# A graph attention layer on one core: twenty places for the turns of the gathers, six of them behind VectorE and ScalarE

## The chip, the cores and the metric

The kernel runs on one core of a Trainium2 chip. A core has TensorE (PE, matrix products; PEld is its weight load), VectorE (DVE), ScalarE (ACT), GpSimd (POOL) and SyncE (SP), each with its own stream of instructions; they wait for each other on semaphores. Sixteen DMA engines move data between HBM and the core's memories, SBUF and PSUM. The metric is the device time of one launch in microseconds (us).

## What is computed

A graph of 12500 nodes with 256 features and 200000 edges, sorted by destination. The layer norm of each node, cut at zero, is `h`. Queries, keys and values with 8 heads are taken from `h`; each edge gets a logit per head, a softmax runs over the edges of a destination, and the weighted values are summed there. A skip product, a GELU, a second layer norm and two residual sums follow.

```python
h = jnp.maximum(_layernorm(x, axis=-1), 0.0)
q = (h @ Wq + bq).reshape(n, HEADS, D)          # k, v alike
logits = jnp.einsum('ehd,ehd->eh', q[dst], k[src]) / jnp.sqrt(jnp.float32(D))
seg_max = jax.ops.segment_max(logits, dst, num_segments=n)
expv = jnp.exp(logits - seg_max[dst])
attn = expv / jax.ops.segment_sum(expv, dst, num_segments=n)[dst]
agg = jax.ops.segment_sum(attn[:, :, None] * v[src], dst, num_segments=n)
out = agg.reshape(n, HID) + (h @ Wskip + bskip)
y = h + jax.nn.gelu(out, approximate=False)
return x + (y - mu) / jnp.sqrt(var + 1e-05) * gamma + beta
```

## The kernel before

A first phase makes `h` and a table `kv_tab` in HBM with a row of 512 numbers for each node, 256 of its key and 256 of its value, and the tables that describe the edges. Then comes the walk over the edges, which takes nearly all of the time. It has NST = 64 steps; a step `c` works on S = 8 streams of edges with K = 3 tiles of 128 edges each (the last step has one tile). The pipeline is written out by hand in one loop body: in the turn of the loop that belongs to step `c`, the last tile of step `c` and the first two of step `c + 1` get their logits, the softmax of step `c` is taken, its values are weighed and added up, and the queries of step `c + 2` are made.

The pieces that the prediction speaks of:

- `turn_windows` (L1493 on TensorE, L1497 on ScalarE) turns the windows of `h` that hold the destinations of a step, and copies them to `hwT`; `queries` (L1511, L1514) multiplies them by the query weights and copies the product to `qw`.
- `spread` (L1585) spreads queries over the edges of a tile, half of its streams at a time, into a PSUM tile with two buffers; `times` (L1596, VectorE) multiplies them with the gathered keys in place; `total` (L1603) sums over a head; `turn` (L1622) transposes the logits; `maxima` (L1634 to L1638) takes the running maxima of the segments and the exponentials.
- `weigh` (L1670, VectorE) multiplies the gathered values by the weights; `hot_n` (L1572, L1575) makes the matrix that sorts edges to nodes, `to_n`; `add_up` (L1693) multiplies the two into sums per node. ScalarE's `taken` (L1716, L1720) copies these out, one group of streams after another.
- `dense` handles one much used group of nodes beside the walk in steps 2 to 50 (L1865 to L1914; its `often` is L1898), and `Pair` finishes 256 nodes in a step, from step 15 on (L1224 to L1335; `shifted` is L1314 and L1317, `scale` is L1321 and L1323). SyncE issues the plain loads and stores.

On each engine the order of the program is kept by `keep`, which hangs every instruction on the one before it on its engine, kept in `latest`. The gathers of GpSimd are not kept so. A tile `(c, j)` of gathered keys and values needs eight of them, one a stream; each is an indirect DMA of 128 rows of `kv_tab`. `gather_next(c, j)` takes a buffer (there are six) for tile `(c + 2, j)` and puts its eight rows on a list, `waiting`. It is called at the start of the loop body for the last tile of the step before, and after `weigh(c, 0)` and `weigh(c, 1)`. A call of `turns` takes rows off the list, in order, and issues each with a semaphore wait on the instruction that it is given: the gather's turn. So a gather can't start before that instruction has ended, and GpSimd, which runs in order, holds all later gathers as well.

Before the change `turns` is called in the pieces themselves, always with TensorE's latest instruction, and the number of rows stands in small tables there: `(1, 2)[part]` in `turn_windows`, `(0, 1)[part]` in `queries`, `(1, 0, 0, 2)[i]` in `hot_e`, `(1, 0, 1)[j]` in `hot_n`, `((1, 1), (1, 2), (1, 1))[j][half]` in `spread`, `(2, 2, 1)[j]` in `turn` and one in each of the three finished groups of `add_up`. In the steady loop that makes turns for just the 24 rows of a step, and two rows of a step's second tile are left for the next step.

Of the kernel before, what the change touches and what calls it, by code (L numbers as in the profile page):

```python
# [37 lines left out]
ACT = mybir.EngineType.Activation  # L38
PE = mybir.EngineType.PE
# [1086 lines left out]
def walk_streams(tc, N, HID, NST, KL, many, ident, idx, d0_row, slot_row, less, near_n, e_tab, at_tab, pen_tab, h_tab,  # L1126
# [268 lines left out]
    with ExitStack() as es:  # L1395
# [90 lines left out]
        def turn_windows(c, part):  # L1486

            g = step[c]
            tiles = (range(1), range(1, 3))[part]
            ps = hot_ps.tile([P, 2, KC, P], F32, name="ps_hot")[:, :len(tiles)]  # L1490
            for r, i in enumerate(tiles):
                for k in range(KC):
                    keep(nc.tensor.transpose(ps[:, :, k, r::2] if part else ps[:, 0, k, :],  # L1493
                                             g["hw"][:, i, k * P:(k + 1) * P], ident))
            turns(latest[PE], (1, 2)[part])
            g["hwT"] = hold.tile([P, 2, KC, P], F32, name="hwT", bufs=1)[:, :len(tiles)]
            keep(nc.scalar.copy(g["hwT"], ps))  # L1497

        def queries(c, part):

            g = step[c]
            if part == 0:
                g["qw"] = hold.tile([P, 3, HID], F32, name="qw")
            tiles = (slice(0, 1), slice(1, 3))[part]
            n = tiles.stop - tiles.start
            ps = hot_ps.tile([P, 2, HID], F32, name="ps_hot")[:, :n]
            keep(nc.tensor.matmul(ps, one_row, twice(b_q3, n), start=True, stop=False,
                                  skip_group_check=True))
            for b in range(n):
                for k in range(KC):  # L1510
                    keep(nc.tensor.matmul(ps[:, b, :], g["hwT"][:, b, k, :], w_q[:, k, :],  # L1511
                                          start=False, stop=k == KC - 1, skip_group_check=True))
            turns(latest[PE], (0, 1)[part])
            keep(nc.scalar.copy(g["qw"][:, tiles, :], ps))  # L1514

        def gather(c, j, behind=None):
# [18 lines left out]
                mybir.DependencyClass.Sync, mybir.DependencyReason.DATA),  # L1535
                reason="turn of the gathers")

        def turns(behind, n=1):

            for _ in range(n):  # L1540
                if waiting:
                    gather_row(*waiting.pop(0), behind)

        def gather_next(c, j):

# [5 lines left out]
        def hot_e(c, i):  # L1551

            g = step[c]
            if i == 0:
                g["to_e"] = hot.tile([P, S // 2, CH], F32, name="to_e")
            turns(latest.get(PE), (1, 0, 0, 2)[i])
            if i % 2:
                t = g["to_e"][:, i - 1:i + 1, :]
                keep(nc.scalar.activation(t, t, AF.Relu, scale=-1.0, bias=ones))  # L1559
                return  # L1560
            for k, pairs in ((0, slice(0, 1)), (1, slice(1, 2))) if i == 0 else ((2, slice(2, 4)),):
                keep(nc.scalar.activation(g["to_e"][:, pairs, :], g["at"][:, pairs, :], AF.Square,  # L1562
                                          bias=less[:, k:k + 1]))

        def hot_n(c, j):

            n = near_n.shape[1]
            if j == 0:
                step[c]["to_n"] = (hot.tile([P, K, n], F32, name="to_n", bufs=1) if c < NST - 1
                                   else done[0].spare(n)[:, None, :])  # L1570
            ps = hot_ps.tile([P, S * WN], F32, name="ps_hot")[:, :n]
            keep(nc.tensor.matmul(ps, step[c]["et"][:, j * P:(j + 1) * P], near_n, start=True,  # L1572
                                  stop=True))
            turns(latest[PE], (1, 0, 1)[j])
            keep(nc.scalar.activation(step[c]["to_n"][:, j, :], ps, AF.Relu, scale=-1.0,  # L1575
                                      bias=ones))

        def spread(c, j, half):

            g = step[c]  # L1580
            ps = qe_ps.tile([P, 2, 2, HID], F32, name="ps_qe")
            for a in range(2):
                for b in range(2):
                    r = slice(b * WN, (b + 1) * WN)
                    keep(nc.tensor.matmul(ps[:, b, a, :],  # L1585
                                          g["to_e"][r, 2 * half + a, j * P:(j + 1) * P],
                                          g["qw"][r, (half + a) * half, :], start=True, stop=True))
            g["qe", half] = ps
            turns(latest[PE], ((1, 1), (1, 2), (1, 1))[j][half])

        def times(c, j, half):

# [22 lines left out]
        def turn(c, j):  # L1615

            g = step[c]
            if c == NST - 1:
                g["xt"] = ag_ps.tile([P, 2 * HID], F32, name="ps_a")
            else:  # L1620
                g["xt"] = logits
            keep(nc.tensor.transpose(g["xt"][:SH, j * P:(j + 1) * P], g["L"][:, j, :], ident))  # L1622
            turns(latest[PE], (2, 2, 1)[j])
            if j == 0:
                keep(nc.scalar.copy(g["xt"][:SH, 0:1],
                                    low0 if c == 0 else step[c - 1]["M"][:, CH - 1:]))
# [52 lines left out]
        def add_up(c, i, tiles=range(K), later=None):  # L1679

            g = step[c]
            streams = [s for s in range(S) if where(s)[0] == i]
            if tiles[0] == 0 and i == 0 and c > NST - 3:
                g["ps", i] = (bank(2)() if c == NST - 2 else logits)[:, :SUMS]
            elif tiles[0] == 0:
                g["ps", i] = (hot_ps.tile([P, 2 * HID], F32, name="ps_hot")
                              if i == 1 or i == 2 and c > NST - 3 else
                              ag_ps.tile([P, 2 * HID], F32, name="ps_a"))[:, :SUMS]
            ps = g["ps", i]
            for j in tiles:  # L1690
                for s in streams:
                    _, at, w = where(s)
                    keep(nc.tensor.matmul(ps[at:at + w, :],  # L1693
                                          g["to_n"][:, j, i * P + at:i * P + at + w],
                                          g["vw"][j][:, s, :], start=j == 0,
                                          stop=j == tiles_of(c) - 1, skip_group_check=True))
            if tiles[-1] < tiles_of(c) - 1:
                return
            turns(latest[PE])
            if later is not None:  # L1700
                later.append((c, i))
            else:
                taken(c, i)
# [343 lines left out]
        for c in range(NST - 1):  # L2047
# [75 lines left out]
                gather_next(c - 1, K - 1)  # L2123
            times(c, K - 1, 0)
            times(c, K - 1, 1)
            if a:
                a.turn()
            if before:
# [2 lines left out]
            if before:  # L2131
                before.shifted()
            total(c, K - 1)
            spread(c + 1, 0, 0)
            spread(c + 1, 0, 1)
            if c == ONCE[1]:
                ending = dense_rows(c)
                next(ending)
            turn_windows(c + 2, 0)
            next(ending, None)  # L2140
            if before:
                before.scale()
                before.store(0)
            turn(c, K - 1)
            if a:
                a.logits()
            behind_exp = []
            if c:
                add_up(c - 1, 0, range(K - 1, K), behind_exp)
            if c:  # L2150
                add_up(c - 1, 1, later=behind_exp)
            if pair:
                pair.turn(later=True)
            maxima(c)
# [4 lines left out]
            turn_back(c)  # L2159
            if c:  # L2160
                add_up(c - 1, 2)
            if a:
                a.top()
                a.exps()
# [3 lines left out]
            if pair:  # L2168
                pair.divisors()
            hot_n(c, 1)  # L2170
            times(c + 1, 0, 0)
            spread(c + 1, 1, 0)
            if a:
# [6 lines left out]
                pair.fetch_x()  # L2180
            times(c + 1, 0, 1)
            hot_n(c, 2)
            total(c + 1, 0)
            if a:
                a.often()
# [2 lines left out]
            if pair:  # L2188
                pair.divide()
            spread(c + 1, 1, 1)  # L2190
            next(ending, None)
            if a:
                a.sums()
# [6 lines left out]
            if pair:  # L2200
                pair.skip(1)
            times(c + 1, 1, 0)
            times(c + 1, 1, 1)
            turn(c + 1, 0)
            spread(c + 1, K - 1, 0)
            queries(c + 2, 0)
            total(c + 1, 1)
            weigh(c, 1)
            gather_next(c, 1)
# [5 lines left out]
            if ahead:  # L2215
                ahead.load()
            turn_windows(c + 2, 1)
            if c + 3 < NST:
                prefetch(c + 3)
            if pair:  # L2220
# [1 line left out]
                table_of(EXP)  # L2222
            next(ending, None)
            turn(c + 1, 1)
            if pair:
                pair.stats(pair.ps)
            weigh(c, K - 1)
            queries(c + 2, 1)
            hot_e(c + 2, 1)
            next(making, None)  # L2230
            spread(c + 1, K - 1, 1)
            hot_e(c + 2, 2)
            if pair:
                pair.root()
# [488 lines left out]
```

## Time and profile before

| | |
|---|---|
| runs | 2621.85, 2622.62, 2644.91 us; median 2622.62 |
| profiled execution | 2633.05 us, its span 2631.5 us |
| granted TensorE clock, mean | 0.853 |
| DMA queue of the gathers (q0): packets, MB, share of 16 engines | 125472, 410.09, 53.2% |
| DMA queue of SyncE (q1): packets, MB, share | 126736, 188.13, 22.8% |
| HBM | 228 GB/s over the span |

The profile is of one execution and somewhat above the median of the runs; sums are made against its own time. Its lines name the line of the kernel, the engine, the operation and the tiles, out<-in. An engine counts as busy while it runs an instruction, not while it waits or issues. Matmuls overlap each other, and their ends in the profile are modelled.

### The profile page before, as it was taken

What the parts mean: (1) busy time and instruction counts of PE and PEld (TensorE: products, weight loads), DVE (VectorE), ACT (ScalarE), POOL (GpSimd) and SP (SyncE); (2) the same over time, 40 slices, a digit from 0 to 9 for tenths busy, and PEclk for the clock granted to TensorE, in tenths of its full rate; (3) what the DMA queues carried; (4) which work ended last, traced back from release to release, by engine and by line L of the source; (5) the groups of instructions that cost most, each with busy time, mean ns of one, the idle gap of its engine ahead of it and who ended that gap; (6) DMA issues with size and microseconds to landing.
All of it is one profiled execution on the core that took longest, in us unless ns stands there. A gap on an engine that the chain in (4) does not pass through costs nothing. (4 is left out here: it accounts for less than half of the span.)

```text
span 2631.5 us, 37655 instructions
## 1 busy us (share of the span) xinstructions
PE 2026.1 (77%) x10723; PEld 1236.4 (47%) x10723; DVE 1905.2 (72%) x2326; ACT 1208.9 (46%) x2667; POOL 1569.9 (60%) x1732
## 2 busy tenths in 40 slices
PE   9994667777777877777787877777777777767776
PEld 4443444444444544554455544544454444444443
DVE  8885766666667777777777777777777776767675
ACT  5662234333333545454545454545454544444443
POOL 5435666666666656666666566565666565666664
PEclk9997787777787889888888888898899888878888
DMA  9786777777767877887787777887788787778773
GB/s 349 292 279 196 211 212 214 213 217 216 213 205 221 232 226 225 234 243 231 230 233 233 232 230 233 242 234 226 235 235 237 229 234 217 226 222 237 225 225 102
DMA packets 253648, 601.84 MB, mean 229 GB/s; under 512 B 53875, under 2 KB 101544, under 8 KB 250486
## 3 DMA queue, kind: packets, MB, share of 16 engines
q0 software_dynamic: 125472, 410.09, 53.2%
q1 hardware_dynamic: 126736, 188.13, 22.8%
q8 instruction: 88, 1.44, 0.2%
q10 hardware_dynamic: 1222, 1.11, 0.1%
q14 instruction: 130, 1.06, 0.1%
HBM read 517.70 MB, written 81.42 MB: 228 GB/s over the span
## 5 line engine op out<-in xcount | busy, mean ns | idle before, releaser
L1531 POOL DMA_INDIRECT kv<-kv_tab,idx x1472 | 1396.7, 949 | 886.5 <-issue 366.0
L1585 PE MATMUL ps_qe<-qw,to_e 64*128 64x256 f32 x3040 | 564.5, 477 | 123.3 <-issue 63.2
L1596 DVE TENSOR_TENSOR kv<-ps_qe,kv 128x1024 f32<-128x1024 f32 x380 | 451.3, 1217 | 171.7 <-remote 65.9
L1585 PEld LDWEIGHTS ps_qe<-qw,to_e 64*128 64x128 f32 x3040 | 359.2, 227 | 297.6 <-issue 196.4
L1670 DVE TENSOR_TENSOR vw<-ps_x,kv 128x2048 f32<-128x2048 f32 x188 | 427.0, 2271 | 56.3 <-ACT to_n L1575 16.6
L1603 DVE TENSOR_REDUCE L<-kv 128x64 f32<-128x2048 f32 x190 | 434.2, 2285 | 4.8
L1693 PE MATMUL ps_a<-vw,to_n 128*32 128x264 f32 (+1 forms) x2232 | 233.7, 434 | 82.9 <-issue 48.4
L1511 PE MATMUL ps_hot<-w_q,hwT 128*128 128x256 f32 x768 | 252.9, 477 | 24.3 <-ACT hwT L1497 11.0
L1514 ACT COPY qw<-ps_hot 128x256 f32<-128x256 f32 (+1 forms) x128 | 61.4, 480 | 433.9 <-issue 125.5
L1511 PEld LDWEIGHTS ps_hot<-w_q,hwT 128*128 128x128 f32 x768 | 165.6, 230 | 77.0 <-issue 22.3
L350 PE MATMUL ps_kv<-w_kv,hT 128*128 128x512 f32 x392 | 184.4, 594 | 0.7 <-ACT hT L264 0.7
L1693 PEld LDWEIGHTS ps_a<-vw,to_n 128*32 128x32 f32 (+1 forms) x2232 | 90.3, 126 | 179.1 <-issue 111.8
L1898 DVE TENSOR_TENSOR kv<-ps_hot,cnt 128x256 f32<-128x256 f32 x49 | 20.8, 425 | 201.7 <-PE ps_hot L1894 136.6
L1720 ACT COPY kv<-ps_a 1x264 f32<-1x264 f32 x372 | 137.3, 369 | 5.5
L1562 ACT ACTIVATE to_e<-at,less 128x384 f32<-128x384 uint8 (+1 forms) x192 | 130.8, 715 | 16.6 <-DMA et<-e_tab 16.6
L1622 PE MATMUL ps_x<-ident,L 128*64 128x128 f32 x189 | 59.6, 315 | 101.6 <-issue 81.4
L1572 PE MATMUL ps_hot<-near_n,et 48*128 48x384 bf16 x190 | 68.7, 386 | 83.9 <-remote 20.5
L1497 ACT COPY hwT<-ps_hot 128x256 f32<-128x256 f32 (+1 forms) x128 | 61.0, 477 | 142.4 <-PE ps_x L1622 59.7
L1435 ACT ACT_TABLE_LOAD x97 | 124.5, 1283 | 2.8 <-issue 1.1
L1575 ACT ACTIVATE to_n<-ps_hot,ones 128x384 f32<-128x384 f32 x189 | 108.2, 576 | 34.2 <-PE ps_hot L1572 24.4
L1693 PE MATMUL ps_hot<-vw,to_n 128*64 128x264 f32 x768 | 120.0, 456 | 3.3 <-issue 2.8
L1559 ACT ACTIVATE to_e<-to_e,ones 128x768 f32<-128x768 f32 x128 | 119.3, 932 | 0.7
(445 smaller groups left out, 2827.4 us busy)
## 6 DMA issues: line engine op xcount, KB each, us to landing
kv<-kv_tab,idx POOLq DMA_INDIRECT x1520
kv_tab<-kvo SPq DMA_DIRECT2D x23, 1024.0 KB
hw<-h_tab SPq DMA_DIRECT2D x256, 64.0 KB
table<-sums_w SPq DMA_DIRECT2D x252, 61.9 KB
group<-h_tab SPq DMA_DIRECT2D x49, 256.0 KB
sums<-table SPq DMA_DIRECT2D x94, 132.0 KB
at<-at_tab SPq DMA_DIRECT2D x64, 192.0 KB
h<-h_tab SPq DMA_DIRECT2D x94, 128.0 KB
```

The source lines that it names most:

```text
L350: nc.tensor.matmul(ps_kv, hT[:, c, :], w_kv[:, c, :], start=c == 0, stop=c == KC - 1)
L1435: keep(nc.scalar.preload_act_table_set(name))
L1511: keep(nc.tensor.matmul(ps[:, b, :], g["hwT"][:, b, k, :], w_q[:, k, :], start=False, stop=k == KC - 1, skip_group_check=True))
L1531: ins = nc.gpsimd.indirect_dma_start(out=t[:, s, :], out_offset=None, in_=kv_tab[:, :], in_offset=bass.IndirectOffsetOnAxis(ap=idx[:, s, j ...
L1559: keep(nc.scalar.activation(t, t, AF.Relu, scale=-1.0, bias=ones))
L1562: keep(nc.scalar.activation(g["to_e"][:, pairs, :], g["at"][:, pairs, :], AF.Square, bias=less[:, k:k + 1]))
L1585: keep(nc.tensor.matmul(ps[:, b, a, :], g["to_e"][r, 2 * half + a, j * P:(j + 1) * P], g["qw"][r, (half + a) * half, :], start=True, stop= ...
L1596: keep(nc.vector.tensor_tensor(k, g["qe", half].rearrange("p b a d -> p a b d"), k, op=OP.mult))
L1603: keep(nc.vector.tensor_reduce(g["L"][:, j, :].rearrange("p (s h) -> p s h", s=S), g["kv"][j][:, :, :HID].rearrange("p s (h d) -> p s h d" ...
L1670: keep(engine.tensor_tensor(t[:, :, HEADS:].rearrange("p s (h d) -> p s h d", h=HEADS), wj[:, :, :, None].to_broadcast([P, t.shape[1], HEA ...
L1693: keep(nc.tensor.matmul(ps[at:at + w, :], g["to_n"][:, j, i * P + at:i * P + at + w], g["vw"][j][:, s, :], start=j == 0, stop=j == tiles_o ...
L1720: keep(copy(step[c + 1]["kv"][0][0:1, s, HID - HEADS:], ps[at:at + 1, :]))
```

## The change

All calls of `turns` leave the pieces and stand in the body of the loop, in twenty places. `turns` now takes the engine and the number, and waits for the latest kept instruction of that engine.

```diff
@@ turn_windows, queries, hot_e, hot_n, spread, turn, add_up
-            turns(latest[PE], (1, 2)[part])
-            turns(latest[PE], (0, 1)[part])
-            turns(latest.get(PE), (1, 0, 0, 2)[i])
-            turns(latest[PE], (1, 0, 1)[j])
-            turns(latest[PE], ((1, 1), (1, 2), (1, 1))[j][half])
-            turns(latest[PE], (2, 2, 1)[j])
-            turns(latest[PE])
...
-        def turns(behind, n=1):
+        def turns(engine, n):
 
             for _ in range(n):
                 if waiting:
-                    gather_row(*waiting.pop(0), behind)
+                    gather_row(*waiting.pop(0), latest[engine])
@@ the loop
                 gather_next(c - 1, K - 1)
             times(c, K - 1, 0)
             times(c, K - 1, 1)
+            turns(DVE, 1)
...
             total(c, K - 1)
+            turns(DVE, 1)
             spread(c + 1, 0, 0)
             spread(c + 1, 0, 1)
...
             turn_windows(c + 2, 0)
+            turns(PE, 1)
+            turns(ACT, 1)
...
             turn(c, K - 1)
+            turns(PE, 1)
...
                 add_up(c - 1, 0, range(K - 1, K), behind_exp)
+                turns(PE, 2)
             if c:
                 add_up(c - 1, 1, later=behind_exp)
+                turns(PE, 1)
...
                 add_up(c - 1, 2)
+                turns(PE, 1)
...
             hot_n(c, 1)
+            turns(ACT, 1)
+            turns(PE, 1)
             times(c + 1, 0, 0)
             spread(c + 1, 1, 0)
...
             times(c + 1, 0, 1)
             hot_n(c, 2)
+            turns(PE, 1)
             total(c + 1, 0)
...
             gather_next(c, 0)
...
             spread(c + 1, 1, 1)
+            turns(PE, 2)
...
             times(c + 1, 1, 0)
+            turns(DVE, 1)
             times(c + 1, 1, 1)
             turn(c + 1, 0)
+            turns(PE, 1)
             spread(c + 1, K - 1, 0)
+            turns(PE, 1)
             queries(c + 2, 0)
+            turns(ACT, 1)
             total(c + 1, 1)
             weigh(c, 1)
             gather_next(c, 1)
...
             turn_windows(c + 2, 1)
+            turns(PE, 1)
...
             turn(c + 1, 1)
+            turns(PE, 2)
...
             queries(c + 2, 1)
+            turns(PE, 2)
...
             spread(c + 1, K - 1, 1)
+            turns(PE, 1)
```

They are numbered here in the order of the loop, 1 to 24, a call for two rows counting as two. Turns 1, 2 and 15 hang on VectorE, 4, 10 and 18 on ScalarE. In the steady loop turns 1 to 4 issue the last four rows of tile `(c + 1, 1)`, 5 to 12 those of `(c + 1, 2)`, 13 to 20 those of `(c + 2, 0)`, and 21 to 24 the first four of `(c + 2, 1)`; four rows are left for the next step instead of two.

## The prediction

> **What bounds the kernel now.** I read the page first, its totals and its groups by line. Columns of a group: busy us, mean ns of one, then the idle time of the engine just before it and what ended most of that.
>
> ```profile
> span 2631.5 us, 37655 instructions
> ...
> PE 2026.1 (77%) x10723; PEld 1236.4 (47%) x10723; DVE 1905.2 (72%) x2326; ACT 1208.9 (46%) x2667; POOL 1569.9 (60%) x1732
> ...
> L1531 POOL DMA_INDIRECT kv<-kv_tab,idx x1472 | 1396.7, 949 | 886.5 <-issue 366.0
> ...
> L1596 DVE TENSOR_TENSOR kv<-ps_qe,kv 128x1024 f32<-128x1024 f32 x380 | 451.3, 1217 | 171.7 <-remote 65.9
> ...
> L1898 DVE TENSOR_TENSOR kv<-ps_hot,cnt 128x256 f32<-128x256 f32 x49 | 20.8, 425 | 201.7 <-PE ps_hot L1894 136.6
> ```
>
> No engine is full. TensorE and VectorE are busy for three quarters and hand work to each other; VectorE's two largest waits are L1596 (171.7 us) and L1898 (201.7 us). GpSimd does nothing in the loop but gathers: 949 ns each, and it sat idle for 886.5 us before them. The question for this change is whether anything waits for a gather. The first reader of gathered data is `times`, L1596, so the second view is that line's own: what VectorE sat idle for before it (us, times).
>
> ```profile
>   remote: 65.9, 17
>   PE ps_qe L1585: 32.5, 10
>   PE ps_hot L1317: 26.7, 8
>   PE ps_hot L1865: 23.2, 9
>   PE ps_a L1693: 13.6, 8
>   issue: 9.3, 4
> ```
>
> These six make 171.2 of the 171.7 us. Four are TensorE, none is a gather or another DMA. "Remote" is a release by a record that the trace lacks; the waits beside it are TensorE's, and I read it so too. So the loop is a ring of TensorE, ScalarE and VectorE, and the gathers run beside it.
>
> **The change, costed in one step.** I lay the new turns over step c = 31 (it begins at 1403.39 us, the next at 1440.13: 36.74 us), from the timeline: start, duration, what.
>
> ```profile
> 1401.06 1.13 PE L1585 MATMUL ps_qe<-qw,to_e 64*128 64x256 f32 x8
> ...
> 1403.39 2.35 DVE L1596 TENSOR_TENSOR kv<-ps_qe,kv 128x1024 f32<-128x1024 f32 x2
> ...
> 1405.77 2.29 DVE L1603 TENSOR_REDUCE L<-kv 128x64 f32<-128x2048 f32 x1
> ...
> 1409.81 0.44 PE L1493 MATMUL ps_hot<-ident,hw 128*128 128x128 f32 x2
> ...
> 1410.08 0.27 PE L1622 MATMUL ps_x<-ident,L 128*64 128x128 f32 x1
> ...
> 1410.35 0.94 POOL L1531 DMA_INDIRECT kv<-kv_tab,idx  x1 [0.31 <-issue]
> 1410.53 0.69 DVE L1321 TENSOR_TENSOR sums<-sums,gam 128x512 f32<-128x512 f32 x1 [2.47 <-ACT sums L1290]
> 1410.55 0.37 ACT L1497 COPY hwT<-ps_hot 128x256 f32<-128x256 f32 x1
> ...
> 1414.17 1.11 PE L1693 MATMUL ps_a<-vw,to_n 128*32 128x264 f32 x8
> ...
> 1415.21 2.78 PE L1693 MATMUL ps_hot<-vw,to_n 128*64 128x264 f32 x12
> ...
> 1419.82 1.56 PE L1693 MATMUL ps_a<-vw,to_n 128*64 128x264 f32 x12 [0.92 <-issue]
> ...
> 1421.31 0.49 PE L1572 MATMUL ps_hot<-near_n,et 48*128 48x384 bf16 x2
> ...
> 1423.71 0.57 ACT L1575 ACTIVATE to_n<-ps_hot,ones 128x384 f32<-128x384 f32 x1
> ...
> 1424.33 0.32 PE L1572 MATMUL ps_hot<-near_n,et 48*128 48x384 bf16 x1 [0.37 <-issue]
> ...
> 1424.34 1.18 PE L1585 MATMUL ps_qe<-qw,to_e 64*128 64x256 f32 x8
> ...
> 1425.42 0.95 POOL L1531 DMA_INDIRECT kv<-kv_tab,idx  x1 [0.30 <-issue]
> ...
> 1427.36 0.95 POOL L1531 DMA_INDIRECT kv<-kv_tab,idx  x1 [0.99 <-issue]
> ...
> 1429.57 2.35 DVE L1596 TENSOR_TENSOR kv<-ps_qe,kv 128x1024 f32<-128x1024 f32 x2
> ...
> 1430.84 1.13 PE L1585 MATMUL ps_qe<-qw,to_e 64*128 64x256 f32 x8 [1.80 <-DVE kv L1596]
> ...
> 1433.28 0.37 ACT L1514 COPY qw<-ps_hot 128x256 f32<-128x256 f32 x1 [2.33 <-issue]
> ...
> 1433.95 0.60 PE L1493 MATMUL ps_hot<-ident,hw 128*128 128x128 f32 x4
> ...
> 1436.49 0.30 PE L1622 MATMUL ps_x<-ident,L 128*64 128x128 f32 x1 [1.95 <-issue]
> ...
> 1437.04 2.66 PE L1511 MATMUL ps_hot<-w_q,hwT 128*128 128x256 f32 x8
> ...
> 1437.24 0.95 POOL L1531 DMA_INDIRECT kv<-kv_tab,idx  x1 [0.30 <-issue]
> ...
> 1439.63 2.08 PE L1585 MATMUL ps_qe<-qw,to_e 64*128 64x256 f32 x8
> ...
> 1440.13 1.21 DVE L1596 TENSOR_TENSOR kv<-ps_qe,kv 128x1024 f32<-128x1024 f32 x1
> ...
> 1442.82 1.23 DVE L1596 TENSOR_TENSOR kv<-ps_qe,kv 128x1024 f32<-128x1024 f32 x1 [1.47 <-PE ps_a L1693]
> ...
> 1453.03 2.36 DVE L1596 TENSOR_TENSOR kv<-ps_qe,kv 128x1024 f32<-128x1024 f32 x2
> ```
>
> *GpSimd's own work:* 24 gathers a step before and after, at 0.95 + 0.30 = 1.25 us from one to the next, 30.0 us of the 36.74. Nothing is added or removed: 0.
>
> *The instructions of the other engines:* none is added, removed or moved; each has the same order. What can differ is which instruction signals. The six new anchors already have readers on other engines (`times` frees the bank of `spread`, `total` feeds `turn`, hwT feeds `queries`, qw feeds `spread`, to_n feeds `add_up`), so I count no new signal; one group of TensorE (`add_up(c, 0, range(2))`) loses its gather. No row shows the price of a signal. Its bounds are one issue gap of 0.30 us a step, as GpSimd's rows have it, gained or lost: 62 steps x 0.30 = 19 us either way. I take 0, by the nearest row: the first of the two `times` at 1403.39 signals TensorE, and the pair takes 2.35 us, no more than two of 1217 ns.
>
> *When the gathers go:* a gather starts 0.30 us after its anchor ends, or 1.25 us after the gather before it. With the ends of the rows above: `times` ends 1405.74, so turn 1 goes at 1406.04; `total` 1408.06, turn 2 at 1408.36; L1493 1410.25, turn 3 at 1410.55; then at 1.25 us turn 4 (the hwT copy ended 1410.92, so it is no bound) 1411.80 and turn 5 1413.05; `add_up` 0 ends 1415.28, turns 6 and 7 at 1415.58 and 1416.83; `add_up` 1 ends 1417.99, turn 8 at 1418.29; `add_up` 2 ends 1421.38, turn 9 at 1421.68; to_n ends 1424.28, turn 10 at 1424.58. Turns 11 to 14 follow at 1425.83, 1427.08, 1428.33 and 1429.58, their anchors done by 1425.52. Turn 15 waits for the first `times` at 1429.57, half of the pair, 1430.75: 1431.05. From there every anchor is done in time (qw 1433.65 for turn 18 at 1434.80; L1622 1436.79 for turn 20 at 1437.30), but for turn 22, L1511 at 1439.70: 1440.00. Turns 23 and 24 go at 1441.25 and 1442.50; the step before left its last in the same way, its L1585 having ended at 1402.19, so that turn 1 above may be up to about 1.3 us later. GpSimd stands still four times instead of in many short gaps, and it catches up.
>
> *Against the old times:* counting gathers from the first, the last row of tile (32, 2) went at 1425.42 and now goes as turn 12 at 1427.08; the first of tile (33, 0) moves from 1427.36 to 1428.33, the eighth from 1437.24 to 1437.30. They are read by L1596 at 1442.82, 1453.03 and about 1454.2. The distances are 15.7, 24.7 and 16.9 us, where the old ones were 17.4, 25.7 and 17.0. How long a gather takes to land no view shows. At the least it is the 0.95 us of its issue; at the most it is below the old 17.4 us, since L1596 waits for none. I take it to be near the lower end, and hidden: the six waits above name no gather in 380 instructions. If that cover were gone, each us late would cost 62 us, one in each step.
>
> [...]
>
> *Sum:* 0, plus or minus 19. The profiled execution took 2633.05 us, 1.5 of it around the span, and stands 10.4 us above the median of the runs, 2622.62. Against the median the forecast is 2622.
>
> **The rivals.**
>
> *Faster: fewer transfers in the long wait.* L1898 waits 4.1 us each time (201.7 / 49), for a chain of ScalarE copies and TensorE groups between about 1417.9 and 1424.0. By the sums above only two gathers start in that stretch, where there were four. If a gather in flight delays that chain by as much as one issue gap, 0.30 us, a step gains 0.6, and 62 steps 37 us: 2585. For it: the wait is the largest of VectorE. Against it: no row shows an engine slowed by a gather.
>
> *Slower: a late gather.* Turn 10 hangs on to_n, behind most of ScalarE's copies; after it GpSimd is behind its turns, by 4.1 us at turn 14 (1429.58 against 1425.52). If a gather needs over 15.7 us to land, VectorE waits at L1596. It decides at 15.7; at 17.4, the upper bound, 1.7 us a step are 105 us: 2728. Against it stands that a tile's rows already spread over 10 us with no wait.
>
> *Slower: crowded transfers of SyncE.* TensorE does wait for a DMA now and then:
>
> ```profile
> PE ps_hot L1314 <- DMA hw<-h_tab: 11.4, 4, 3.2
> ```
>
> That is 2.85 us a time, in 4 steps of the 47 with a pair. If the runs of gathers behind turns 10 to 24 push these loads back, so that 12 more steps wait, it costs 34 us: 2656.
>
> *Slower: GpSimd and VectorE shut each other out.* Turn 2 starts right behind `total`, so that its gather often meets L1321, which reads two operands of SBUF. If the two exclude each other, a step loses at most the 0.69 of L1321: 45 steps, 31 us, 2653. The rows at 1410.35 and 1410.53 speak against it: they overlap now, and take 0.94 and 0.69, as elsewhere. [...]
>
> **How the numbers follow.** A measurement of this kernel tells about 1% from no change, 26 us, so "the same" is 2596 to 2649. The forecast, gathers that move by under 2 us where 15 are free, gets 0.60. The faster rival gets 0.25: L1898 is the largest wait, and half a gap more for each gather would carry its price well past the edge. The three slower ones get 0.05 (a late gather), 0.06 (crowding) and 0.04 (the shut-out). The time is that of the likeliest, 2622. Its own range with the 19 us is 2603 to 2641. The range given reaches past the price of the faster rival, 2585, by 5 us, and to the crowding's 2656: 2580 to 2656. Outside are about 0.11 of the faster one, the late gather and some of the crowding, 0.18 together. Faster by over 1%: 0.25; slower by over 1%: 0.15; same: 0.60.
>
> **What would show it right or wrong.** Right: GpSimd's gathers 1472 at 949 ns with idle time near 886 us, in fewer and longer gaps, ended by L1596, L1603 and ScalarE lines as well; L1596 with about 170 us of idle time before it and no gather among its releasers; L1898 still near 4.1 us each. The faster rival shows as L1898 falling to some 3.5 us each, the late gather as L1596 waiting for kv, the crowding as L1314 or L1317 waiting for a DMA in many steps, the shut-out as L1321 over 687 ns. Wrong altogether would be a change of the step by more than 0.4 us with none of these.

## The result, and the profile after

The changed kernel takes 2640.99 us (median of 20 runs, 2632.90 to 2649.74), the kernel before 2625.84 us (20 runs beside it, 2617.25 to 2644.91): a ratio of 1.0055, 95% interval 1.0040 to 1.0071. That is some 15 us slower, inside the range given and inside "the same" by its bound of 1%, but it is a loss, and none was forecast. The profiled execution took 2642.64 us. Its page, with the lines that answer to those of before (L1531, L1596 and L1898 are now L1529, L1591 and L1891):

```profile
span 2641.1 us, 37779 instructions
...
PE 2075.6 (79%) x10723; PEld 1260.6 (48%) x10723; DVE 1906.1 (72%) x2326; ACT 1206.4 (46%) x2667; POOL 1571.4 (59%) x1732
...
L1529 POOL DMA_INDIRECT kv<-kv_tab,idx x1472 | 1398.4, 950 | 898.4 <-issue 393.7
...
L1591 DVE TENSOR_TENSOR kv<-ps_qe,kv 128x1024 f32<-128x1024 f32 x380 | 451.0, 1216 | 128.4 <-remote 47.0
...
L1891 DVE TENSOR_TENSOR kv<-ps_hot,cnt 128x256 f32<-128x256 f32 x49 | 20.8, 425 | 186.6 <-PE ps_hot L1887 90.8
```

VectorE does the same work, and its two largest waits are shorter, by 43.3 us (171.7 to 128.4) and 15.1 us (201.7 to 186.6). So the loss isn't there. VectorE's idle time as a whole is 8.4 us longer, for other waits have grown: L1321 from 26.8 to 58.5 us, L1267 from 51.3 to 74.1, L1670 (now L1664) from 56.3 to 71.4 and L1634 (now L1628) from 52.6 to 74.7. The first `times` of steps 0, 15, 51 and 62 in the timeline (start, duration) say in which steps it is; before, then after:

```profile
258.41 1.23 DVE L1596 TENSOR_TENSOR kv<-ps_qe,kv 128x1024 f32<-128x1024 f32 x1 [0.42 <-PE ps_a L1783]
...
799.58 1.22 DVE L1596 TENSOR_TENSOR kv<-ps_qe,kv 128x1024 f32<-128x1024 f32 x1
...
2154.57 1.22 DVE L1596 TENSOR_TENSOR kv<-ps_qe,kv 128x1024 f32<-128x1024 f32 x1
...
2563.47 1.21 DVE L1596 TENSOR_TENSOR kv<-ps_qe,kv 128x1024 f32<-128x1024 f32 x1
```

```profile
254.93 1.22 DVE L1591 TENSOR_TENSOR kv<-ps_qe,kv 128x1024 f32<-128x1024 f32 x1 [0.46 <-PE ps_a L1776]
...
796.86 1.22 DVE L1591 TENSOR_TENSOR kv<-ps_qe,kv 128x1024 f32<-128x1024 f32 x1
...
2164.71 1.22 DVE L1591 TENSOR_TENSOR kv<-ps_qe,kv 128x1024 f32<-128x1024 f32 x1
...
2575.54 1.22 DVE L1591 TENSOR_TENSOR kv<-ps_qe,kv 128x1024 f32<-128x1024 f32 x1
```

The 62 steps take 2305.1 us before and 2320.6 after, 15.5 more (the spans differ by 9.6 us only, for what lies ahead of the steps and behind them is 5.9 us shorter); steps 15 to 50 alone, where dense groups and pairs both run, 1355.0 and 1367.8, 12.9 more or 0.36 us a step. In these steps a wait has grown that the prediction didn't look at: ScalarE's copy of the dense group's transposes (L1871, now L1864), and behind it VectorE's L1321, which needs ScalarE's next instruction, L1290. By the views of these two lines: duration in ns (least, median, most), then the idle time of the engine before them (us, times), before and then after:

```profile
L1871 ACT COPY kv<-ps_hot x49: 562/586/587, 337.3 to 2122.4; 128x512 f32<-128x512 f32 x49
...
  PE ps_qe L1585: 34.8, 15
  remote: 29.1, 9
  PE ps_hot L1317: 4.3, 4
...
L1321 DVE TENSOR_TENSOR sums<-sums,gam x45: 679/683/694, 884.3 to 2536.0; 128x512 f32<-128x512 f32 x45
...
  ACT sums L1290: 24.4, 14
```

```profile
L1864 ACT COPY kv<-ps_hot x49: 561/586/588, 333.4 to 2136.2; 128x512 f32<-128x512 f32 x49
...
  remote: 147.9, 38
  PE ps_x L1617: 12.3, 4
...
L1321 DVE TENSOR_TENSOR sums<-sums,gam x45: 676/683/724, 878.7 to 2547.1; 128x512 f32<-128x512 f32 x45
...
  ACT sums L1290: 57.2, 17
```

ScalarE stands still before the copy for 68.4 us before (with 0.2 of a fourth releaser) and 160.5 us after (with 0.3). What it waits for is TensorE, and TensorE's records don't show why. One step of the timeline after:

```profile
1440.43 1.13 PE L1581 MATMUL ps_qe<-qw,to_e 64*128 64x256 f32 x8
...
1442.53 0.66 PE L1858 MATMUL ps_hot<-ident,group 128*128 128x128 f32 x4
...
1443.94 0.49 ACT L1860 ACTIVATE kv<-cnt,ones 128x256 bf16<-128x256 int16 x1
...
1446.03 1.22 DVE L1591 TENSOR_TENSOR kv<-ps_qe,kv 128x1024 f32<-128x1024 f32 x1 [2.05 <-PE ps_hot L1317]
...
1446.92 0.59 ACT L1864 COPY kv<-ps_hot 128x512 f32<-128x512 f32 x1 [2.49 <-remote]
```

By their record the transposes end at 1443.19; ScalarE is free at 1444.43, and yet starts the copy only at 1446.92, just behind an update of TensorE's semaphore that the trace has at 1446.90. VectorE's second `times` of the step needs the `spread` that is recorded from 1440.43 to 1441.56, and it too starts only at 1446.03, so the delay isn't the copy's own. TensorE's results come after its records end, here by 3.71 us (1446.90 against 1443.19): over the 49 copies the median from the last transpose's record to the copy is 4.41 us, and 3.52 in the kernel before. This wait, 160.5 against 68.4 us, is the mark by which the experiments are read below.

The built programs differ in one more thing than the prediction said. TensorE has 2304 matrix products that update a semaphore in the trace before, and 2096 after: not only `add_up(c, 0, range(2))` lost its signal (52 times), but also `spread(c + 1, 0, 0)`, `spread(c + 1, 0, 1)` and `spread(c + 1, 1, 0)` (156), since only gathers had waited for these just there. VectorE and ScalarE signal as often as before.

### The profile page after: what moved, and what is told of

It reads as the page before. It is cut to its first block, busy times and chain, and to the rows that moved or that the text cites. A ratio compares the mean times of both kernels' runs of the same rounds, so it can differ in the third digit from the quotient of the medians.

```text
span 2641.1 us, 37779 instructions
## 1 busy us (share of the span) xinstructions
PE 2075.6 (79%) x10723; PEld 1260.6 (48%) x10723; DVE 1906.1 (72%) x2326; ACT 1206.4 (46%) x2667; POOL 1571.4 (59%) x1732
## 5 line engine op out<-in xcount | busy, mean ns | idle before, releaser
L1529 POOL DMA_INDIRECT kv<-kv_tab,idx x1472 | 1398.4, 950 | 898.4 <-issue 393.7
L1591 DVE TENSOR_TENSOR kv<-ps_qe,kv 128x1024 f32<-128x1024 f32 x380 | 451.0, 1216 | 128.4 <-remote 47.0
L1581 PEld LDWEIGHTS ps_qe<-qw,to_e 64*128 64x128 f32 x3040 | 351.2, 219 | 301.6 <-issue 238.5
L1664 DVE TENSOR_TENSOR vw<-ps_x,kv 128x2048 f32<-128x2048 f32 x188 | 427.1, 2272 | 71.4 <-ACT to_n L1571 26.7
L1598 DVE TENSOR_REDUCE L<-kv 128x64 f32<-128x2048 f32 x190 | 434.2, 2285 | 4.8
L1891 DVE TENSOR_TENSOR kv<-ps_hot,cnt 128x256 f32<-128x256 f32 x49 | 20.8, 425 | 186.6 <-PE ps_hot L1887 90.8
L1619 ACT COPY ps_x<-M 64x1 f32<-64x1 f32 x62 | 9.7, 156 | 276.2 <-PE ps_x L1617 127.9
L1687 PE MATMUL ps_hot<-vw,to_n 128*64 128x264 f32 x768 | 128.5, 479 | 8.8 <-issue 4.7
L1255 PE MATMUL ps_a<-w_s,hT 128*128 128x256 f32 x368 | 129.8, 514 | 0.0
```

The costliest lines, as they stand in the source:

```text
L1255: self.keep(nc.tensor.matmul(self.ps[:, b, :], self.hT[:, b, c, :], w_s[:, c, :], start=False, stop=False, skip_group_check=True))
L1529: ins = nc.gpsimd.indirect_dma_start(out=t[:, s, :], out_offset=None, in_=kv_tab[:, :], in_offset=bass.IndirectOffsetOnAxis(ap=idx[:, s, j ...
L1581: keep(nc.tensor.matmul(ps[:, b, a, :], g["to_e"][r, 2 * half + a, j * P:(j + 1) * P], g["qw"][r, (half + a) * half, :], start=True, stop= ...
L1591: keep(nc.vector.tensor_tensor(k, g["qe", half].rearrange("p b a d -> p a b d"), k, op=OP.mult))
L1598: keep(nc.vector.tensor_reduce(g["L"][:, j, :].rearrange("p (s h) -> p s h", s=S), g["kv"][j][:, :, :HID].rearrange("p s (h d) -> p s h d" ...
L1664: keep(engine.tensor_tensor(t[:, :, HEADS:].rearrange("p s (h d) -> p s h d", h=HEADS), wj[:, :, :, None].to_broadcast([P, t.shape[1], HEA ...
```

## The experiments

Theories at the start: *signals* (the four lost signals of TensorE), *anchors* (the turns on VectorE or on ScalarE), *moved gathers* (the times at which the transfers start). Each group of runs stood beside runs of the kernel before on the same chip.

**First group** (the kernel before at 2629.40 us). `e1_signals` gives the four signals back, by a memset on GpSimd behind each group; `e2_memsets` has the memsets without the wait.

```diff
+        def mark(dep=True):
+
+            ins = nc.gpsimd.memset(spot, 0.0)
+            if dep:
+                tc.add_manual_dep(ins.ins, latest[PE], ...)
@@ the loop; e2_memsets: mark(False)
             spread(c + 1, 0, 0)
+            mark()
             spread(c + 1, 0, 1)
+            mark()
...
             spread(c + 1, 1, 0)
+            mark()
...
             add_up(c, 0, range(K - 1))
+            mark()
```

> The changed kernel with one more short GpSimd instruction (a memset of one number) behind each of four TensorE groups a step, spread(c+1,0,0), spread(c+1,0,1), spread(c+1,1,0) and add_up(c,0,range(2)), hung on that group, so that the group signals again as in the kernel before; the gathers keep the changed kernel's turns. Theory 'signals' (these four lost signals of TensorE are what changed the step): back to about 2626 us, ratio 1.000. Theory 'anchors' (the six turns on VectorE and ScalarE) and theory 'moved gathers' (the times at which transfers start): as the changed kernel, about 2641 us, ratio 1.0055, and not faster than e2_memsets.

> The changed kernel with the same four memsets on GpSimd at the same places, hung on nothing: the price of the memsets alone. All three theories: as the changed kernel, about 2641 us, ratio 1.0055. If the four instructions on GpSimd delay something by themselves: above 2645 us.

Measured: `e1_signals` 2642.65 us, 1.0050 (1.0034 to 1.0065); `e2_memsets` 2667.51 us, 1.0144 (1.0126 to 1.0162). `e2_memsets` isn't the control that it was meant to be. Its memsets, hung on nothing, did not run at the places where the text has them, but in the first steps, all before 339 us; those of e1 ran through the whole walk. The view of their line, e1, then e2 (duration in ns; first and last start in us):

```profile
L1545 POOL MEMSET spot<- x248: 88/89/92, 274.9 to 2576.5; 1x1 f32 x124
```

```profile
L1545 POOL MEMSET spot<- x248: 88/89/90, 226.1 to 338.6; 1x1 f32 x124
```

What e2 takes more lies there (last section). From the first `times` of step 3 to that of step 62 it takes 2210.8 us, the changed kernel 2211.7 and e1 2211.3, the kernel before 2196.5. So e1, with its four signals back, is as slow as the changed kernel. That speaks against *signals*, unless the memsets inside the walk cost what the signals bring; no run shows their price there.

`e3_before_minus` is the kernel before, with the turns of these four groups moved to neighbours on TensorE:

```diff
-            turns(latest[PE], (1, 2)[part])
+            turns(latest[PE], (3, 2)[part])
-            turns(latest.get(PE), (1, 0, 0, 2)[i])
+            turns(latest.get(PE), (1, 0, 0, 0)[i])
-            turns(latest[PE], (1, 0, 1)[j])
+            turns(latest[PE], (1, 0, 2)[j])
-            turns(latest[PE], ((1, 1), (1, 2), (1, 1))[j][half])
+            turns(latest[PE], ((0, 0), (0, 2), (1, 3))[j][half])
```

> The kernel before, with the five turns of these four TensorE groups given to other TensorE pieces that signal anyway (two to turn_windows, one to hot_n, two to the last spread): TensorE then has exactly the changed kernel's signals, every turn still hangs on TensorE, and no gather moves by more than about 4 us. Theory 'signals': about 2641 us, ratio 1.0055. Theory 'anchors': 2626 us, ratio 1.000. Theory 'moved gathers': 2626 us or a little off either way, since few gathers move.

Measured: 2634.99 us, 1.0029 (1.0010 to 1.0047), between what *signals* and *anchors* said. Half of the loss, without any turn on VectorE or ScalarE. `e4_all_pe` is the changed kernel with `turns(DVE, 1)` and `turns(ACT, 1)` made `turns(PE, 1)`:

> The changed kernel with its six turns on VectorE and ScalarE hung on TensorE's latest instruction at the same places. One of the four lost signals, that of add_up(c,0,range(2)), comes back with it, the three of spread don't. Theory 'anchors': about 2626 us, ratio 1.000. Theory 'signals': most of the loss stays, about 2637 us, ratio 1.004. Theory 'moved gathers': about 2641 us.

Measured: 2625.45 us, 0.9979 (0.9966 to 0.9992), as *anchors* said, and not the 1.004 of *signals* or the 1.0055 of *moved gathers*. The new places alone cost nothing; with all turns on TensorE they are a little better than the old ones.

**Second and third group.** Four kernels were to part VectorE's turns, ScalarE's turns and the signal of `add_up`:

```diff
@@ e5_dve_to_pe (1, 2, 15); e6_act_to_pe the same with ACT (4, 10, 18)
-            turns(DVE, 1)
+            turns(PE, 1)
@@ e7_all_pe_no_signal: e4_all_pe, and turn 1 on the last spread
+            if waiting:
+                gather_row(*waiting.pop(0), last_spread if c else latest[PE])
@@ e8_add_up_signal: turn 24 behind add_up
             spread(c + 1, K - 1, 1)
-            turns(PE, 1)
...
             add_up(c, 0, range(K - 1))
+            turns(PE, 1)
```

> The changed kernel with only the three turns on VectorE (1, 2 and 15) hung on TensorE's latest instruction; the three on ScalarE stay. Turn 1 then hangs on add_up(c,0,range(2)), which signals again. Theory 'VectorE anchors' (GpSimd waiting for VectorE at the start of a step makes the loop longer): 2626 us, ratio 0.998 to 1.000. Theory 'ScalarE anchors': 2641 us, ratio 1.0055. Theory 'signal of add_up': 2626 us.

> The changed kernel with only the three turns on ScalarE (4, 10 and 18) hung on TensorE's latest instruction; the three on VectorE stay, and add_up(c,0,range(2)) doesn't signal. Theory 'VectorE anchors': 2641 us, ratio 1.0055. Theory 'ScalarE anchors': 2626 us, ratio 0.998 to 1.000. Theory 'signal of add_up': 2641 us.

> All twenty-four turns on TensorE as in e4_all_pe, but turn 1 hangs on the last spread of the step before in place of add_up(c,0,range(2)), so that this group doesn't signal: TensorE has the changed kernel's signals and no turn hangs on VectorE or ScalarE. Theories of the anchors: as e4_all_pe, 2625 us, ratio 0.998. Theory 'signal of add_up': as the changed kernel, 2641 us, ratio 1.0055.

> The changed kernel with its last turn of a step moved from behind the last spread to behind add_up(c,0,range(2)), some 1 us later: that group signals again, the six turns on VectorE and ScalarE stay. Theory 'signal of add_up': as e4_all_pe, 2625 us, ratio 0.998. Theories of the anchors: 2641 us, ratio 1.0055.

Measured: 0.9994, 1.0002, 1.0006 and 1.0002, each within 0.0012. They part nothing, for here the kernel before takes 2188.04 us, 17% less than in the first group. So the changed kernel itself was run next, and three of the four again:

> The changed kernel itself, run beside the kernel before once more, because the last four runs came from a chip on which the kernel before takes 2188 us and not 2626. If this run is on a chip with about 2626 us, where TensorE's results come up to 5 us after its records end: ratio 1.0055 again. If it is on one with about 2188 us, where VectorE and GpSimd hardly stand still: theory 'TensorE's slow state' (the change only costs where TensorE is late) says 1.000, within 0.15%; a theory by which the turns themselves cost 0.25 us a step, whatever the chip, says 1.007.

Measured: 2187.07 us against 2187.17, 0.9995 (0.9980 to 1.0010). `f2_dve_to_pe`, `f3_act_to_pe` and `f4_no_signal`, the repeats of e5, e6 and e7 with the same expectations, gave 0.9994, 1.0003 and 1.0001 (1.000 within 0.15% was expected here). Here the change costs nothing. The page and the lines of `f1_after` show what is different:

```profile
PE 1803.6 (83%) x10723; PEld 1131.1 (52%) x10723; DVE 1899.1 (87%) x2326; ACT 1204.9 (55%) x2667; POOL 1574.0 (72%) x1732
...
L1529 POOL DMA_INDIRECT kv<-kv_tab,idx x1472 | 1398.2, 950 | 452.9 <-issue 248.6
L1591 DVE TENSOR_TENSOR kv<-ps_qe,kv 128x1024 f32<-128x1024 f32 x380 | 453.7, 1217 | 84.8 <-PE ps_qe L1581 42.5
```

```profile
L1864 ACT COPY kv<-ps_hot x49: 559/563/587, 314.5 to 1767.6; 128x512 f32<-128x512 f32 x49
...
  PE ps_hot L1858: 1.4, 2
```

GpSimd's gathers and VectorE's `times` take as long as before (950 and 1217 ns), and VectorE, ScalarE and GpSimd are busy for the same time within 0.4%; only TensorE is quicker, and the copy waits 1.4 us in all in place of 160.5. GpSimd goes from gather to gather in (1398.2 + 452.9) / 1472 = 1.26 us, where 0.95 and the gap of 0.30 make 1.25: it hardly stands still (14 of the 1472 gaps are over 0.35 us), and 24 gathers, some 30 us, are the step (62 steps take 1867.0 us). A turn's instruction is then nearly always done before its gather can go. And here `times` does wait for gathers, by the view of L1591 (us, times):

```profile
  DMA kv<-kv_tab,idx: 40.0, 34
```

In the first profile of the changed kernel GpSimd takes (1398.4 + 898.4) / 1472 = 1.56 us from gather to gather. So there are two settings of one kernel, one in which TensorE is prompt and GpSimd is the bound, one bound by late TensorE, and the change costs only in the second. What makes the setting isn't known: two groups, one of each kind, bear the same chip number.

**The remaining runs** each parted what was left. VectorE's three turns on TensorE, ScalarE's kept:

> The same kernel as e5_dve_to_pe once more: VectorE's three turns on TensorE, ScalarE's three kept. On a chip with about 2626 us before: theory 'VectorE anchors' 0.998 to 1.000 (the loss goes with these three), theory 'ScalarE anchors' 1.0055 (the loss stays), a part of each: between 1.001 and 1.004. On a chip with about 2188 us: 1.000 within 0.15%.

Measured: 2603.92 us against 2607.23, 0.9987 (0.9968 to 1.0007). ScalarE's turns are struck out: all three are kept, and nothing is lost. But the edit also gave `add_up` its signal, and it moved the first gathers. `g4_early_dve` keeps VectorE and was to move the time alone (`turn_on(i)` issues one gather behind instruction `i`):

```diff
+            old = latest[DVE]
             times(c, K - 1, 0)
+            first = latest[DVE]
             times(c, K - 1, 1)
-            turns(DVE, 1)
+            turn_on(old)
...
             total(c, K - 1)
-            turns(DVE, 1)
+            turn_on(first)
```

(and turn 15 in the same way).

> The changed kernel with VectorE's three turns hung on earlier instructions of VectorE: turn 1 on the last weigh of the step before, turn 2 on the first times(c,K-1,0), turn 15 on what stands before times(c+1,1,0). They still wait for VectorE, and add_up(c,0,range(2)) doesn't signal, but the gathers may go 1 to 3 us earlier, about when they go in g1_dve_to_pe. On a chip with about 2610 us before: theory 'late gathers at the start of the step' (their time counts, not the engine they wait for) 0.998 to 1.000; theory 'a wait for VectorE costs by itself' and theory 'signal of add_up' 1.0055. On a chip with about 2188 us: 1.000 within 0.15%.

It (1.0002, 0.9992 to 1.0012) and, beside it, a further run of e7's kernel, `g5_no_signal` (1.0000, 0.9988 to 1.0012), fell where the kernel before takes 2189.78 us, so it was run again:

> The same kernel as g4_early_dve once more, since that one ran on a chip where there is no loss to take away: VectorE's three turns on earlier instructions of VectorE, no signal of add_up(c,0,range(2)), gathers 1 to 3 us earlier. On a chip with about 2610 us before: theory 'late gathers at the start of the step' 0.998 to 1.000; theories 'a wait for VectorE costs by itself' and 'signal of add_up' 1.0055. On a chip with about 2188 us: 1.000 within 0.15%.

Measured: 2658.99 us against 2625.30, 1.0118 (1.0080 to 1.0156). Less moved than was expected. Counted from the first `times` of a step (medians of steps 15 to 49), turns 1 and 2 go at 4.79 and 7.08 us in the changed kernel, at 4.82 and 6.07 in h1, and at 5.55 and 7.52 in g1. So only turn 2 is earlier in h1, and it is slower still; in g1 both are later, and it loses nothing. Gathers that come too late at the start of a step are struck out. Left were the wait for VectorE and the signal. e8's kernel gives the signal back and keeps VectorE's turns:

> The same kernel as e8_add_up_signal: the changed kernel with only its last turn of a step moved from behind the last spread to behind add_up(c,0,range(2)), so that this group signals again; all six turns on VectorE and ScalarE stay. On a chip with about 2610 us before: theory 'signal of add_up' 0.998 to 1.000, and ScalarE's copy of the dense group (L1864) begins some 3.5 us after TensorE's last record of it, as in the four kernels so far where the group signals (3.5 to 3.7), and not 4.4 to 5.1 us as in the three where it doesn't. Theory 'a wait for VectorE costs by itself': 1.0055. On a chip with about 2188 us: 1.000 within 0.15%.

Measured: 2626.52 us against 2626.54, 1.0000 (0.9978 to 1.0022). e7's kernel takes the signal away and has no turn on VectorE:

> The same kernel as e7_all_pe_no_signal: all twenty-four turns on TensorE as in e4_all_pe (0.9979), turn 1 on the last spread of the step before, so that add_up(c,0,range(2)) doesn't signal. On a chip with about 2610 us before: theory 'signal of add_up' 1.003 to 1.012, with ScalarE's copy of the dense group 4.4 us or more behind TensorE's last record of it; theory 'a wait for VectorE costs by itself' 0.998, as no turn waits for VectorE here. On a chip with about 2188 us: 1.000 within 0.15%.

Measured: 2622.05 us against 2626.42, 0.9984 (0.9971 to 0.9998). Both theories fall in their plain form: VectorE's turns cost nothing in h2, and h3 has the changed kernel's signals (2097, one more) and no loss. The copy starts 3.04 us (median) behind the last transpose's record in h2, and 3.54 in h3, where some 3.5 and 4.4 or more were expected. The copy's waits in h1, h2 and h3, by the view of its line:

```profile
L1869 ACT COPY kv<-ps_hot x49: 562/586/587, 334.3 to 2148.9; 128x512 f32<-128x512 f32 x49
...
  remote: 169.2, 39
  PE ps_x L1622: 7.8, 3
  PE ps_hot L1493: 6.1, 1
```

```profile
L1864 ACT COPY kv<-ps_hot x49: 563/586/590, 334.0 to 2120.7; 128x512 f32<-128x512 f32 x49
...
  remote: 49.8, 25
  PE ps_hot L1317: 10.8, 7
  PE ps_hot L1858: 3.4, 5
```

```profile
L1864 ACT COPY kv<-ps_hot x49: 560/585/586, 331.0 to 2116.5; 128x512 f32<-128x512 f32 x49
...
  remote: 65.8, 26
  PE ps_hot L1317: 12.0, 6
  PE ps_x L1617: 9.7, 4
```

They sum to 183.1, 64.0 and 87.5 us. All ten kernels where TensorE is late, by this mark. The second column says for which TensorE group GpSimd waits between the last `spread` of a step and `turn_windows` of the next:

| kernel | TensorE group waited for | copy's wait, us | ratio |
|---|---|---|---|
| e4_all_pe | add_up, L1317 | 55.6 | 0.9979 |
| h2_add_up_signal | add_up | 64.0 | 1.0000 |
| before | add_up, two of spread | 68.4 | 1 |
| g1_dve_to_pe | add_up, L1317 | 69.3 | 0.9987 |
| e1_signals (memsets) | add_up, two of spread | 87.0 | 1.0050 |
| h3_no_signal | L1317 | 87.5 | 0.9984 |
| e3_before_minus | none | 135.3 | 1.0029 |
| after | none | 160.5 | 1.0055 |
| e2_memsets (memsets) | none | 175.3 | 1.0144 |
| h1_early_dve | none | 183.1 | 1.0118 |

The waits are of one profiled execution each (that of e3, at 2647.32 us, is the second longest of its twelve), the ratios of all runs. The four without such a wait have the longest waits of the copy, and all four lose. Of the six with one, five lose nothing. `e1_signals` has the wait and a short copy's wait, and loses 0.50%; either its memsets cost that, which no run shows, or it speaks against the reading. This reading was found after the runs. No run was made to test it, and no row shows how a wait of GpSimd can make TensorE's results come sooner. It says what to try: the changed kernel with turn 2 alone behind L1317 should lose nothing. That wasn't tried.

`e4_all_pe` has the lowest ratio, 0.9979 where TensorE is late; g1 and h3 are not told apart from it. It was not run where TensorE is prompt; its nearest kin there, e7, had 1.0006, 1.0001 and 1.0000.

## Why the prediction was wrong, point by point

**The bound.** "No engine is full", a ring of TensorE, ScalarE and VectorE with the gathers beside it: that holds for the profile it was read from. It isn't the kernel's own: at 2187 us GpSimd is full (1.26 us from gather to gather, where issue and gap make 1.25), and `times` waits for gathers (40.0 us in `f1_after`). Where it did so in `f1_after`, it began 3.75 to 8.40 us after the last of its four gathers had started. That is a measure, in that setting, of the landing that the prediction took to be near the 0.95 us of the issue.

**Instructions and times.** As forecast, the gathers are 1472 at 950 ns (forecast: 949), GpSimd idles 898.4 us (forecast: near 886), and L1598 is among the releasers of its gathers:

```profile
  DVE L L1598: 39.8, 32
```

No gather is among the releasers of L1591 in this profile. Not as forecast, L1591 waits 128.4 us (forecast: about 170), and GpSimd's gaps are not fewer and longer: 416 are over 0.35 us, where there were 340, and 58 over 2 us, where there were 69. Nor was GpSimd's own work unchanged: it waits on a semaphore 1290 times before its gathers, where it did so 1166 times. h2 has as many instructions (37779) and loses nothing, so this isn't the loss.

**The step that failed** is "the gathers run beside the ring": that a turn may be hung on anything, because 15.7 us of slack lie behind a gather. The slack is there. But where TensorE is late, the choice of a turn changes when TensorE's results come (the copy starts 3.04 us behind the last transpose's record in h2 and 4.41 in the changed kernel, medians), whether by the wait, the signal or the time that go with it: h2 and the changed kernel differ in one turn of 24, and their ratios, 1.0000 and 1.0055, have intervals that don't meet. These two stood in different groups, each beside the kernel before; within one group, on one chip, e3 and e4 have all their turns on TensorE, in different places, and their ratios, 1.0029 and 0.9979, don't meet either. How the choice of a turn does this stays open. The sum looked for the cost at the reader of the gathers; it came, by VectorE's and ScalarE's waits, at L1864, L1321 and L1628, none of which waits for a gather. L1267 waits longer too, but no less in kernels without loss (82.3 us in e4, 87.4 in h2).

**Signals.** "One group loses its gather" missed three groups. The bound set on it, 19 us either way, would have held the loss, but missing signals alone don't make the loss: h3 lacks the same ones but for one, and loses nothing.

**The rivals.** Faster: L1898 fell, from 4.1 to 186.6 / 49 = 3.8 us each (3.5 was its sign), and the 15.1 us went into other waits. Late gather: no. Crowded transfers: no; the view of waits after has no L1314 that waits for a DMA, where there were 11.4 us. GpSimd and VectorE shutting each other out: VectorE isn't held, for L1321 has a median of 683 ns in both; it was late, not long. But GpSimd takes longer: in the changed kernel 33 gathers start while L1321 runs, and their median is 1147 ns, where that of all gathers is 946 ns (before, 13 gathers did, with 986 ns). One of them:

```profile
1449.49 0.68 DVE L1321 TENSOR_TENSOR sums<-sums,gam 128x512 f32<-128x512 f32 x1
...
1449.84 1.15 POOL L1529 DMA_INDIRECT kv<-kv_tab,idx  x1 [1.38 <-DVE L L1598]
```

That is some 0.2 us for each of 33 gathers, 7 us in all, on an engine that stands still for 898.

**The edge "0.4 us".** The prediction would have called a step that changes by over 0.4 us with none of its signs wrong altogether. The steps that lose lost 0.36 on average, by waits that were on no list.

## What to carry to other kernels

Where an engine's results come after its records end (here the copy starts 4.41 us behind the record, the median), a profile's slack doesn't say that a wait beside it is free: before a turn or an order is moved off that engine, look at the first reader behind it and count its idle time in both kernels. A synchronisation edge is part of the change even if no instruction of the other engines moves: list which groups lose their waiter (here four, and TensorE's updates went from 2304 to 2096). An instruction that is put in as a control has to be looked up in the trace: that of e2 ran elsewhere than it was written. And a difference of half a per cent belongs to the setting in which it was measured; here it was 0.55% in one and nothing in the other.

## What the runs showed of the hardware

The same kernel takes 2607 to 2629 us in some groups of runs and 2187 to 2190 in others, with VectorE, ScalarE and GpSimd busy for the same time within 0.4% (the changed kernel in its first profile and in `f1_after`). TensorE's busy time in the records is 2075.6 against 1803.6 us for the same 10723 matrix products. In the prompt setting the copy starts as soon as ScalarE is done with the instruction before it, at 1220.63, where the record of its transposes ends at 1219.67:

```profile
1219.01 0.66 PE L1858 MATMUL ps_hot<-ident,group 128*128 128x128 f32 x4
...
1220.23 0.49 ACT L1860 ACTIVATE kv<-cnt,ones 128x256 bf16<-128x256 int16 x1
...
1220.63 0.56 ACT L1864 COPY kv<-ps_hot 128x512 f32<-128x512 f32 x1
```

The granted clock goes with the setting (0.928 in `f1_after`, 0.834 in the changed kernel's first profile, whose trace has 135 stretches at half clock), but doesn't order the kernels within one. Of the ten profiled executions where TensorE is late, that of `h2_add_up_signal` has the lowest, 0.820, with a ratio of 1.0000; that of `e3_before_minus`, which loses, has 0.842.

The 248 memsets of one number on GpSimd made e2 0.9% slower than the changed kernel (1.0144 against 1.0055), by where they ran. 106 of them stand before the first `times` of step 0, and 66 of these in one stretch, between two gathers:

```profile
226.11 9.62 POOL L1545 MEMSET spot<- 1x1 f32 x66
```

The first `times` of steps 0 and 3 in `e2_memsets`, and that of step 3 in the changed kernel (its step 0, at 254.93, stands above):

```profile
259.32 1.23 DVE L1600 TENSOR_TENSOR kv<-ps_qe,kv 128x1024 f32<-128x1024 f32 x1 [6.29 <-issue]
...
387.89 1.22 DVE L1600 TENSOR_TENSOR kv<-ps_qe,kv 128x1024 f32<-128x1024 f32 x1
```

```profile
363.84 1.22 DVE L1591 TENSOR_TENSOR kv<-ps_qe,kv 128x1024 f32<-128x1024 f32 x1
```

Step 0 begins 4.4 us later, and the next three steps take 128.6 us against 108.9. That is 24.1 us in all, more than the 21.0 us between the two spans; behind the last memset the steps go at the changed kernel's pace.
